# Four-block sequence model on one core: where the attention loop issues its strip matmuls, its maxima's transposes and its variances, and where the first expert tile's tokens lie

## The chip, the core and the metric

The kernel runs on one core of a Trainium2 chip. TensorE multiplies (PE, with PEld for its weight loads), VectorE (DVE) and ScalarE (ACT) do elementwise work and read PSUM, GpSimd (POOL) does elementwise work on SBUF and starts indirect DMAs, SyncE (SP) starts the other DMAs. Each engine takes its instructions in order; semaphores tie the engines to each other. The metric is the device time of one execution in microseconds, the median of three runs. All numbers are float32, so each matmul is recorded as two passes of TensorE (a transpose as one).

## What is computed

The input is `x` with 4 sequences of 512 tokens and 288 features, and one condition vector per sequence. Four blocks follow each other:

```python
x = x + ((z @ expm(A(cond))) - z) @ U.T           # z = x @ U, U from the QR of P
for block in (L1, L2, L3):                         # 16 heads of 18 features
    h = layernorm(x) * (1 + scale) + shift
    q, k, v = split(h @ Wqkv + bqkv)               # L2 also normalises each head of q and k
    x = x + gate * (softmax(q @ k.T * 18**-0.5) @ v @ Wproj + bproj)
    h = layernorm(x) * (1 + scale2) + shift2
    x = x + gate2 * mlp(h)                         # L3: the best 2 of 4 experts, weighted
```

The heads of L2 are normalised over their 18 features, so its q and k need a variance per head. L3's experts work on 19 tiles of 256 tokens, collected by routing.

## The kernel before

**Batches and steps.** The three attention blocks times four sequences make 12 batches, numbered n = 0 to 11 (n = 4 to 7 are L2, n = 8 to 11 L3). `attend(n, ...)` (L1207) runs 32 steps for a batch: 4 groups G of 4 heads, 8 steps s each. A step issues, in this order:

1. `maxima(ahead, mstep)` (L1119): four score matmuls (two heads, two passes each) into `p_s`, and on DVE a `tensor_reduce` to the row maxima `M`. It runs `LOOK = 10` steps ahead of the rest, so in step 22 of a batch it begins on the next batch's Q and K; in step 5 of a group it does the last piece (mstep 7) of the next group.
2. `weigh(G, s)` (L1139): the transposed scores of the present group into `p_st`, and the exponential on ACT. `p_s` and `p_st` share a PSUM tag of two buffers, so the next `p_s` can start once the last reduce is done.
3. in even steps `give_values()` (L1237): `p_av`, exponentials times values.
4. filling work: `left` grows by `total / 32`, plus 0.5 in odd steps and minus 0.5 in even ones; while it is positive, the next piece of the generator `fill` is issued and its cost is taken off.

Scores and the strip matmuls use 32 of the array's rows, so matmuls on different strips run side by side; `p_av` uses 128 rows and 32 columns, the rest all 128 rows.

`take_maxima(G + 1)` (L1130) transposes `M` on PE (four transposes into `p_m`; the last needs the reduces of msteps 6 and 7) and subtracts the result on DVE from Q (in the extra row that each head's Q has behind its 18 features). It is issued in step 6 of a group, between `weigh` and `give_values`.

**The filling work of batch n** is, in order: `project(n + 1)` (L1044) up to the point where it yields `None`; `finish(n - 1)` (L1180), the four output projections `p_o` with their gated additions; the rest of `project(n + 1)`; the transposes `p_t` for the MLP of batch n - 1; in batches 10 and 11 routing pieces. What is left in `fill` at the end of the 32 steps is issued there. After the steps, `mlp(n - 1)` runs.

`project` has nine jobs, five for q and k (`p_qk`, m = 0 to 4) and four for v (`p_v`), taken in pairs. A pair issues its dense matmuls (two blocks of 128 features), then the pending evictions of the pair before (`later`), then its two strip matmuls (the last 32 features, called tails here), then its first evictions. For L2 an eviction has three parts: square (ACT) and bias (DVE); `p_var` with logarithm and exponential (ACT); the scaling on DVE (`stage<-stage,qn_g,tmp`), the shift on POOL and the DMA to DRAM (`qd`). After the tails of qk 4 and v 0 come twelve DMAs: `qd` is read back into the padded Q and K of batch n + 1 (eight), and four zero rows. These DMAs are on SP's queue, in order with the transfers of attention's outputs (`o` to `od`), of the sums and of weights. Both q and k are read head by head with a stride of four, so each of K's four transfers contains rows of job m = 4; Q's four end with job m = 2.

PSUM tag `mm` has three buffers for `p_qk`, `p_v`, `p_var`, `p_m`, `p_o`, `p_t`. The SBUF tag `stage` has three buffers and `o`, attention's sums on their way to DRAM, three.

**After attention** two pools for the experts take the place of the pool `attn`. `tokens_T(0)` (L1427) transposes the first 256 tokens into `hTe`; `tile_pieces(t)` yields four times per tile, and at each yield `rest()` gets one slot: `slot(gen)` advances the routing of sequences 2 and 3 (`route`, L858) until a piece with a cost of 1.0 or more. All routing there is DVE chains with a few small matmuls (`p_r`, `p_logit`, `p_pos`, `p_T`).

Of the kernel before, what the change touches and what calls it, by code (L numbers as in the profile page):

```python
# [9 lines left out]
F32 = mybir.dt.float32  # L10
# [6 lines left out]
B, T, C = 4, 512, 288  # L17
NT = 4
KC, KP = 3, 96

KW, TAIL, STRIPS = 2, 32, 3
H, HD, HS = 16, 18, 32
VS = HD + 1
NG = 4
# [14 lines left out]
TS = 256  # L39
# [8 lines left out]
def cond_seq_kernel(ctx: ExitStack, tc: tile.TileContext, a: dict, out: bass.AP):  # L48
# [802 lines left out]
    def route(b):  # L851
# [23 lines left out]
        for j in range(NT):  # L875
            for k in range(KW + 1):
                r = slice(0, 128 if k < KW else TAIL)
                matmul(p[:, j * NE:(j + 1) * NE], h[r, k, j * 128:(j + 1) * 128], R["wg"][r, k, :],
                       start=(k == 0), stop=(k == KW))
            if j % 2:  # L880
                yield 1.6
        lg, rank, m, gt, ge, mx = (R[n] for n in ("lg", "rank", "m", "gt", "gte", "mx"))
        vector.tensor_copy(lg.rearrange("p j e -> p (j e)"), p[:, :n16])
        S4 = [128, NT, NE, NE]
# [33 lines left out]
        for j in range(NT):  # L918
            q = slice(j * NE, (j + 1) * NE)
            vector.tensor_tensor(low[:, q], wide(lo[:, q].rearrange("p (n o) -> p n o", o=1), [128, NE, 128]),  # L920
                                 wide(R["iota128"].rearrange("p (o k) -> p o k", o=1), [128, NE, 128]), ALU.is_equal)
            yield 0.6

        vector.tensor_mul(lg, lg, m)
        vector.tensor_reduce(mx, lg, AX.X, ALU.add)
# [102 lines left out]
    with tc.tile_pool(name="attn", bufs=2) as at:  # L1028
# [14 lines left out]

        def project(n, norm):  # L1044

            l, b = divmod(n, B)
            wqk, wv = WA[l][:2]
            h = hT[0]
            yield from layernorm(l, 0, b, h, norm)
            qd = scratch.tile([2 * H, HD, T], F32, tag="qd", name=f"qd{n}")  # L1050
            flat = qd.rearrange("h d t -> (h d) t")

            def qk_job(m):
                w = min(QP, QK - m * QP)
                cols = slice(m * QP, m * QP + w)
                p = pmm(f"p_qk{n}_{m}")

                def evict():
                    bias = QB[l][0:w, m:m + 1]
                    t = at.tile([QP, T], F32, tag="stage", name=f"stage{n}_{m}", bufs=3)[0:w]  # L1060
                    if l != 1:
                        scalar.activation(t, p[0:w], AF.Identity, bias=bias, scale=scol[0:w, m:m + 1])
                    else:
                        tmp = at.tile([128, 2, T], F32, tag="e", name=f"tmp{n}_{m}", bufs=6)
                        sq, rs = tmp[0:w, 0, :], tmp[0:w, 1, :]
                        scalar.activation(sq, p[0:w], AF.Square, bias=bias)
                        vector.tensor_scalar(t, p[0:w], bias, None, ALU.add)
                        yield 0.0
                        pv = pmm(f"p_var{n}_{m}")
                        matmul(pv[0:w], varsel.rearrange("p h d -> p (h d)")[0:w, 0:w], sq, start=True, stop=True)  # L1070
                        scalar.activation(rs, pv[0:w], AF.Ln, bias=eps5[0:w])
                        scalar.activation(rs, rs, AF.Exp, scale=-0.5)
                        yield 0.86
                        vector.scalar_tensor_tensor(t, t, gains[0][0:w, m:m + 1], rs, ALU.mult, ALU.mult)
                        nc.gpsimd.tensor_scalar(t, t, gains[1][0:w, m:m + 1], None, ALU.add)
                    dma(flat[cols], t)
                return p[0:w], 0.86, lambda k, r: (wqk[r, k, cols], h[r, k, :]), evict

            def v_job(j):
                p = pmm(f"p_v{n}_{j}")  # L1080

                def evict():
                    (scalar.copy if j % 2 else vector.tensor_copy)(
                        V[n % 2][:, j, :, 0:HD], p[:, :C].rearrange("p (h d) -> p h d", d=HD))
                    yield from ()
                return p[:, :C], 0.49, lambda k, r: (h[r, k, j * 128:(j + 1) * 128], wv[r, k, :]), evict

            jobs = [(qk_job, m) for m in range(NQ)] + [(v_job, j) for j in range(NT)]
            later = []
            for i in range(0, len(jobs), 2):  # L1090
                pair = []
                for job, arg in jobs[i:i + 2]:
                    p, cost, operands, evict = job(arg)
                    for k in range(KW):
                        matmul(p, *operands(k, slice(0, 128)), start=(k == 0), stop=False)
                        yield cost
                    pair.append((p, operands, evict))
                for e in later:
                    yield from e
                for q, (p, operands, evict) in enumerate(pair):  # L1100
                    matmul(p, *operands(KW, strip(q)), start=False, stop=True)

                later = [e for e in [evict() for p, operands, evict in pair] if next(e, None) is not None]
                yield 0.95
                if i <= NQ - 1 < i + 2:
                    for e in later:
                        yield from e
                    later = []

                    src = qd.rearrange("(s g i) d t -> s i d g t", s=2, i=4)  # L1110
                    for s, t in enumerate((Q[n % 2], K[n % 2])):
                        for q in range(4):
                            dma(t[q * HS:q * HS + HD], src[s, q])
                    for q in range(4):
                        dma(Q[n % 2][q * HS + HD:q * HS + VS], zero_row[q:q + 1].rearrange("a (g t) -> a g t", t=T))
                    there.add(n)
                    yield None

        def maxima(G, step):  # L1119
# [86 lines left out]

        def attend(n, fill, total, norms):  # L1207

            left = 0.0
            for step in range(8 * NG):  # L1210
                g, s = divmod(step, 8)
                G = NG * n + g
                ahead, mstep = divmod(8 * G + s + LOOK, 8)
                if ahead < NG * NB:
                    while ahead // NG not in there:
                        next(fill)
                    maxima(ahead, mstep)
                E.append(weigh(G, s))
                if s == 8 - 2 and G + 1 < NG * NB:
                    take_maxima(G + 1)  # L1220
                if s % 2 == 0:
                    give_values()
                left += total / (8 * NG) + (0.5 if s % 2 else -0.5)
                next(norms, None)
                while left > 0:
                    cost = next(fill, "end")
                    if cost == "end":
                        break
                    left -= cost or 0.0
                if s % 2:  # L1230
                    ready.append((G, s // 2))
            for _ in fill:
                pass
            for _ in norms:
                pass

        def give_values():  # L1237

            if not ready:
                return  # L1240
            G, c = ready.pop()
            if c == 0:
                PO[0] = pacc(f"p_av{G}")
            sum_values(G, PO[0], c, E[:2])
            del E[:2]
            if c == NT - 1:
                t = at.tile([128, T], F32, tag="o", name=f"o{G}", bufs=3)
                scalar.copy(t, PO[0])
                n, g = divmod(G, NG)
                if g == 0:  # L1250
                    S[n] = (scratch.tile([H, T], F32, tag="sd", name=f"sd{n}"),
                            scratch.tile([H, HD, T], F32, tag="od", name=f"od{n}"))
                dma(S[n][0][4 * g:4 * g + 4, :], t.rearrange("(h r) c -> h r c", r=HS)[:, HD])
                for h in range(4):
                    dma(S[n][1][4 * g + h], t[h * HS:h * HS + HD])
# [55 lines left out]
        for t in range(LOOK):  # L1311
            maxima(*divmod(t, 8))
            if t == 8:
                take_maxima(0)
            next(rest, None)
            next(new)
            if t == 5:
                projection_bias(0)
        for n in range(NB):
# [70 lines left out]
    with tc.tile_pool(name="moe", bufs=1) as pool, tc.tile_pool(name="moe2", bufs=2) as pool2:  # L1390
# [34 lines left out]
                gather(g, xtab if t >= EARLY else xtab[0:2 * T], idx[:, 2 * t + h:2 * t + h + 1])  # L1425

        def tokens_T(t):  # L1427
            h = HT[t] = pool2.tile([128, KW + 1, TS], F32, tag="hTe", name=f"hTe{t}")
            p, q = pmm(f"p_te{t}"), pmm(f"p_tf{t}")
            for i in range(2):  # L1430
                cols = slice(i * 128, (i + 1) * 128)
                for k in range(KW):
                    transpose(p[:, k * TS + i * 128:k * TS + (i + 1) * 128], XG[t, i][:, k * 128:(k + 1) * 128], ident)
                transpose(q[:XW - KW * 128, cols], XG[t, i][:, KW * 128:XW], ident)
            vector.tensor_copy(h[:, 0:KW].rearrange("p k n -> p (k n)"), p)
            scalar.copy(h[:XW - KW * 128, KW], q[:XW - KW * 128, :TS])

        def tile_pieces(t):
# [118 lines left out]
```

## Time and profile before

| | us |
|---|---|
| median of the three runs | 2061.03 (2056.3 to 2065.32) |
| the profiled execution | 2073.42 |
| its span on the core | 2071.7 |
| DVE busy, of it `TENSOR_REDUCE store<-p_s` x384 | 928.4, 470.3 |
| ACT busy, of it `ACTIVATE e<-p_st` x384 | 783.6, 392.7 |
| granted TensorE clock, mean | 0.954 |

The profiled execution is one run with the recorder on; views of its trace (timeline, waits, windows) count microseconds from its first instruction. PE's busy time is near the whole span in any case, since matmul records overlap; what a stage is bound by shows in the waits and the timeline. The first 213 us hold the rotation of block 0 and the first projections, the steps run from there to about 1655 us, the expert tiles from there to the end. The batches (first `p_st` to first `p_st` of the next) take between 86.9 us (n = 0, no MLP in it) and 143.2 us (n = 5).

### The profile page before, as it was taken

Reading aid. Unit: us, or ns where it says so; the run is one execution under the profiler, and the core shown is the slowest. Engines: PE = TensorE matmul, PEld = TensorE weight load, DVE = VectorE, ACT = ScalarE, POOL = GpSimd, SP = SyncE. Lnnn points to the kernel's source line nnn. Section 1 sums busy time; section 2 is a strip of 40 time slices with the busy share of each in tenths; the row PEclk is TensorE's granted clock in tenths of the full one; section 3 lists DMA queues with packets and bytes.
Section 4 is the critical chain, followed back from the end, with each engine's and each line's share of the span. In section 5 each row is a group of like instructions: output and inputs, shape, how many; then the busy total and the mean of one; then the engine's idle time right before and its main releaser. Section 6 shows DMA issues by size and latency. Waiting matters only on the chain. (4 is left out here: it accounts for less than half of the span.)

```text
span 2071.7 us, 26248 instructions
## 1 busy us (share of the span) xinstructions
PE 1887.7 (91%) x10269; PEld 935.6 (45%) x10269; DVE 928.4 (45%) x1953; ACT 783.6 (38%) x1169; POOL 251.9 (12%) x362
## 2 busy tenths in 40 slices
PE   6769879999999999899999999998987888999998
PEld 4544223343523434234234353333332266788886
DVE  6764646346164362552644626345576234211111
ACT  5122454444254343453544434434444222221221
POOL 1000010001010020010100000000000122233232
PEclk9578999999999999999999999999999689999999
DMA  3212152031131221511213112161212265576673
GB/s 97 71 40 62 36 147 84 22 89 36 25 85 30 70 62 42 136 42 54 72 26 77 42 54 81 21 134 35 83 46 66 86 222 167 182 242 200 211 241 97
DMA packets 89419, 187.23 MB, mean 90 GB/s; under 512 B 25453, under 2 KB 50456, under 8 KB 86802
## 3 DMA queue, kind: packets, MB, share of 16 engines
q1 hardware_dynamic: 77462, 103.39, 19.1%
q0 software_dynamic: 11248, 79.79, 11.9%
q10 hardware_dynamic: 584, 2.36, 0.3%
q8 instruction: 81, 1.33, 0.3%
q14 instruction: 44, 0.36, 0.1%
HBM read 152.49 MB, written 55.45 MB: 100 GB/s over the span
## 5 line engine op out<-in xcount | busy, mean ns | idle before, releaser
L60 ACT ACTIVATE e<-p_st 128x1024 f32<-128x1024 f32 x384 | 392.7, 1023 | 650.7 <-PE p_st L60 646.3
L60 DVE TENSOR_REDUCE store<-p_s 128x2 f32<-128x1024 f32 x384 | 470.3, 1225 | 364.5 <-PE p_st L60 320.7
L60 PE MATMUL p_s<-store 32*128 32x512 f32 x1536 | 442.2, 648 | 82.5 <-DVE store L60 81.3
L60 PE MATMUL p_st<-store 32*128 32x512 f32 x1536 | 445.7, 659 | 0.9 <-DVE store L60 0.9
L60 PEld LDWEIGHTS p_s<-store 32*128 32x128 f32 x1536 | 120.0, 185 | 315.3 <-DVE store L60 228.2
L60 PE MATMUL p_av<-e,store 128*32 128x512 f32 x1536 | 212.8, 627 | 2.2 <-ACT e L60 2.2
L60 PE MATMUL p_he<-hTe,store 128*128 128x256 f32 (+1 forms) x1026 | 188.4, 390 | 4.2 <-DVE hTe L60 4.2
L60 PE MATMUL p_ye<-store,hide 128*128 128x288 f32 x684 | 171.4, 409 | 0.0
L60 PEld LDWEIGHTS p_he<-hTe,store 128*128 128x128 f32 (+1 forms) x1026 | 151.4, 191 | 37.7 <-issue 13.6
L695 POOL TENSOR_TENSOR x<-x,gated 128x288 f32<-128x288 f32 x80 | 63.9, 799 | 841.6 <-DVE gated L60 841.6
L60 PE MATMUL p_qk<-hT,wqk 128*126 128x512 f32 (+1 forms) x360 | 163.1, 622 | 0.3 <-DVE store L60 0.3
L60 ACT ACTIVATE hide<-p_he,store 128x256 f32<-128x256 f32 x171 | 68.5, 478 | 245.1 <-PE p_he L60 244.3
L60 PE MATMUL p_h<-hT,w 128*128 128x512 f32 (+1 forms) x432 | 153.5, 610 | 5.2 <-DVE store L60 5.2
L60 PEld LDWEIGHTS p_ye<-store,hide 128*128 128x128 f32 x684 | 128.2, 190 | 36.7 <-ACT hide L60 2.3
L60 PE MATMUL p_y<-w,hid 128*128 128x288 f32 x576 | 141.8, 407 | 0.0
L60 DVE TENSOR_TENSOR gated<-p_y,gate 128x288 f32<-128x288 f32 x32 | 14.6, 457 | 283.0 <-PE p_y L60 283.0
L60 PEld LDWEIGHTS p_y<-w,hid 128*128 128x128 f32 x576 | 108.8, 190 | 35.5 <-issue 6.1
L60 PEld LDWEIGHTS p_st<-store 32*128 32x128 f32 x1536 | 118.2, 187 | 12.1 <-issue 9.1
L60 PEld LDWEIGHTS p_h<-hT,w 128*128 128x128 f32 (+1 forms) x432 | 62.1, 189 | 95.1 <-issue 84.9
L60 PE MATMUL p_o<-wp,oc 126*128 126x288 f32 (+1 forms) x288 | 99.4, 468 | 1.3 <-DVE oc L60 1.3
L60 PEld LDWEIGHTS p_qk<-hT,wqk 128*126 128x126 f32 (+1 forms) x360 | 47.1, 178 | 95.9 <-issue 94.3
L60 DVE COPY hTe<-p_te 128x512 f32<-128x512 f32 x19 | 13.1, 690 | 169.2 <-PE p_tf L60 117.8
(248 smaller groups left out, 1728.8 us busy)
## 6 DMA issues: line engine op xcount, KB each, us to landing
store<-qd SPq DMA_DIRECT2D x96, 144.0 KB
qd<-stage SPq DMA_DIRECT2D x48, 252.0 KB
od<-o SPq DMA_DIRECT2D x192, 36.0 KB
rd<-rd SPq DMA_DIRECT2D x12, 576.0 KB
oc<-od SPq DMA_DIRECT2D x24, 252.0 KB
rb<-rd SPq DMA_DIRECT2D x24, 252.0 KB
etab<-in_L_cond_w_dram SPq DMA_DIRECT2D x4, 1296.0 KB
etab<-in_L_cond_w_dram SPq DMA_DIRECT2D x8, 576.0 KB
```

The lines of the kernel that those rows point to most:

```text
L60: ins = f(*args, **kw)
L695: nc.gpsimd.tensor_add(x[b][:, j, :], x[b][:, j, :], t)
```

## The change

- `project` yields the word "strips" ahead of its tails. `attend` stops filling there, and issues the tails in the next step, right behind `weigh` and ahead of `give_values`.
- `take_maxima(G + 1)` moves from step 6 (behind `weigh`) to step 5, behind its filling work; `left` is reduced by 0.6 in such a step.
- For L2 (`l == 1`) the pending evictions of qk 4 are no longer drained at once behind its tails: the drain and the twelve DMAs (`send`) come one pair later, behind the dense matmuls of v 1 and v 2.
- `stage` has four buffers, `o` two.
- `hTe0` lies in a buffer of `wqk` in place of the experts' pool.
- In `route`, for sequences 2 and 3, the first half of the logits costs 0.8 and the last piece of `low` 1.0.

```diff
@@ route
             if j % 2:
-                yield 1.6
+                yield 0.8 if b >= 2 and j < NT - 1 else 1.6
@@
-            yield 0.6
+            yield 1.0 if b >= 2 and j == NT - 1 else 0.6
@@ project
-                    t = at.tile([QP, T], F32, tag="stage", name=f"stage{n}_{m}", bufs=3)[0:w]
+                    t = at.tile([QP, T], F32, tag="stage", name=f"stage{n}_{m}", bufs=4)[0:w]
@@
+            def send():
+
+                src = qd.rearrange("(s g i) d t -> s i d g t", s=2, i=4)
+                for s, t in enumerate((Q[n % 2], K[n % 2])):
+                    for q in range(4):
+                        dma(t[q * HS:q * HS + HD], src[s, q])
+                for q in range(4):
+                    dma(Q[n % 2][q * HS + HD:q * HS + VS], zero_row[q:q + 1].rearrange("a (g t) -> a g t", t=T))
+                there.add(n)
@@
                 for e in later:
                     yield from e
+                if l == 1 and i <= NQ + 1 < i + 2:
+                    send()
+                    yield None
+                yield "strips"
                 for q, (p, operands, evict) in enumerate(pair):
                     matmul(p, *operands(KW, strip(q)), start=False, stop=True)
 
                 later = [e for e in [evict() for p, operands, evict in pair] if next(e, None) is not None]
                 yield 0.95
-                if i <= NQ - 1 < i + 2:
-                    for e in later:
-                        yield from e
-                    later = []
...
+                if l != 1 and i <= NQ - 1 < i + 2:
+                    send()
                     yield None
@@ attend
-            left = 0.0
+            left, strips = 0.0, False
@@
                 E.append(weigh(G, s))
-                if s == 8 - 2 and G + 1 < NG * NB:
-                    take_maxima(G + 1)
+                if strips:
+                    left -= next(fill)
+                    strips = False
                 if s % 2 == 0:
                     give_values()
-                left += total / (8 * NG) + (0.5 if s % 2 else -0.5)
+                take = s == 7 + 8 - LOOK and G + 1 < NG * NB
+                left += total / (8 * NG) + (0.5 if s % 2 else -0.5) - (0.6 if take else 0.0)
                 next(norms, None)
                 while left > 0:
                     cost = next(fill, "end")
-                    if cost == "end":
+                    strips = cost == "strips"
+                    if cost == "end" or strips:
                         break
                     left -= cost or 0.0
+                if take:
+                    take_maxima(G + 1)
                 if s % 2:
                     ready.append((G, s // 2))
@@ give_values
-                t = at.tile([128, T], F32, tag="o", name=f"o{G}", bufs=3)
+                t = at.tile([128, T], F32, tag="o", name=f"o{G}", bufs=2)
@@ tokens_T
-            h = HT[t] = pool2.tile([128, KW + 1, TS], F32, tag="hTe", name=f"hTe{t}")
+            if t:
+                h = pool2.tile([128, KW + 1, TS], F32, tag="hTe", name=f"hTe{t}")
+            else:
+                h = wattn.tile([128, KW + 1, QK], F32, tag="wqk", name="hTe0")[:, :, 0:TS]
+            HT[t] = h
@@
-            vector.tensor_copy(h[:, 0:KW].rearrange("p k n -> p (k n)"), p)
+            vector.tensor_copy(h[:, 0:KW], p.rearrange("p (k n) -> p k n", k=KW))
```

More of the change, by code (lines that the diff above doesn't have):

```diff
@@ L1104, in project @@
                 yield 0.95
-                if i <= NQ - 1 < i + 2:
-                    for e in later:
-                        yield from e
-                    later = []
[L1110 to L1116, printed above, removed]
+                if l != 1 and i <= NQ - 1 < i + 2:
+                    send()
                     yield None
@@ L1315, in cond_seq_kernel @@
             next(rest, None)
-            next(new)
+            if next(new) == "strips":
+                next(new)
             if t == 5:
```

## The prediction

> **What bounds the kernel now.** I read the page's busy shares and slices first, then the waits of PE, then the timeline of single steps.
>
> ```profile
> PE 1887.7 (91%) x10269; PEld 935.6 (45%) x10269; DVE 928.4 (45%) x1953; ACT 783.6 (38%) x1169; POOL 251.9 (12%) x362
> PE   6769879999999999899999999998987888999998
> PEclk9578999999999999999999999999999689999999
> ```
>
> PE is nearly full from slice 6 to the end, and its clock sags around slices 32 and 33 (1605 to 1710 us). So any stall of PE goes straight to the end. The waits of PE from 480 to 1640 us (total, times, longest):
>
> ```profile
> PE p_s L60 <- DVE store L60: 62.2, 90, 3.8
> PE p_t L60 <- DVE xn L60: 6.5, 7, 1.1
> ```
>
> The score matmuls wait for the reduce of the step before. The timeline of PE in batch 7 gives the rhythm (start, busy, engine):
>
> ```profile
> 1111.72 0.70 PE L60 MATMUL p_s<-store 32*128 32x512 f32 x2
> ...
> 1114.18 0.70 PE L60 MATMUL p_s<-store 32*128 32x512 f32 x2 [0.32 <-DVE store L60]
> ...
> 1115.34 1.98 PE L60 MATMUL p_qk<-hT,wqk 128*126 128x512 f32 x4
> 1117.26 0.70 PE L60 MATMUL p_s<-store 32*128 32x512 f32 x2
> ```
>
> From 1111.72 to 1114.18 is 2.46 us: scores 1.07 us, reduce 1.23, hand-overs. That is the floor of a step. The next step has two dense `p_qk` and takes 3.08: PE bound. **A step takes the larger of 2.46 us and the sum of its PE rows.** From starts in the timeline: scores 1.07, a dense 512-column matmul 0.86 (two passes of 0.429), `p_av` 1.06, `p_o` 1.84, a pair of tails behind scores 0.86, behind dense work 1.05, and a change of array shape about 0.2 (the next pass starts 0.522 after the last in place of 0.429, and the second pass 0.53 after the first). Walking all 32 steps of batch 4 so gives 127.6 us against 132.8 in the trace; the rest are waits that stand in the timeline one by one (variances, `xn`, the gap ahead of the MLP).
>
> **Steps.** I put the program order of both kernels through that rule. The change spreads unevenly: when "strips" ends an odd step's filling, that step is left at the floor with about 1.4 us of PE unused, and the next, even step carries tails, `p_av` and dense work. Batch 7 by the rule: steps 11 to 15 were 2.9 + 2.5 + 2.6 + 3.4 + 3.8 and become 2.5 + 3.9 + 2.7 + 2.5 + 2.5, which gains 1.1; but steps 20 to 27, 4.0 + 2.5 + 3.3 + 2.7 + 2.7 + 2.2 + 2.7 + 2.2, become 4.0 + 2.7 + 4.0 + 2.5 + 2.7 + 2.7 + 2.5 + 2.6, which loses 1.4, and the other steps lose 1.5 (0.3 in 0 to 10, 0.5 in 16 to 19, 0.7 after the last score step). The transposes cost 0.2 above the floor in both places: in step 6 as 1.07 + 0.6 + 1.0, in step 5 because the last of the four waits for that step's own reduce. The 0.6 taken off in four steps per batch leaves a piece (`p_t`) for the end. Differences of the sums: batch 0 +0.5; 1, 2 +1.9 each; 3 to 6 +3.5 each; 7, 8 +1.7 each (rounded rows above: 1.8); 9 +0.4; 10 +0.7; 11 +2.0. **Sum +24.8.** Taken back: the last `p_t` now fill the gap in which the MLP's first matmul waited 0.9 for a reduce, 8 x 0.9 = -7.2; waits for `xn` shrink 4 x 0.4 = -1.6.
>
> Here a rule can be set against the rows. The Trainium skill, "TensorEngine Tiling (Array Packing)", Tiling Modes, says that a change of tiling mode drains TensorE. The row agrees (0.2 us). In the program order there are 1147 such changes before and 1125 after. By the rule alone 22 x 0.2 = -4.4 us; by the steps, +24.8, since most removed changes lie in steps that wait for DVE anyway. I take the steps.
>
> **Variances (batches 3 to 6).** In step 9 both `p_var` stood together, the second 1.05 us behind its PSUM buffer; steps 14 to 16 lost about 1.45 more, with DVE behind two scalings and two evictions. Both pairs are now steps apart: 4 x -2.5 = -10. Against it, `p_v` 1 and 2 hold two of the three `mm` buffers during `p_o`, so the second `p_o` of step 23 waits for a 0.45 us eviction: 4 x 0.75 = +3. In batch 5 the DVE queue stood at `oc<-oc,rb`, then at a full `stage`, PE idled 3.75 us and the clock fell: 143.2 against 132.8 us. With `var` 1 a step earlier and four `stage` buffers I leave 1.5 of these 10.7: -9.2. Two `o` buffers cost nothing: the DMAs of one leave within 3 us of its copy, and a group lasts about 22; without that cover ACT's copy, with all exponentials behind it, would wait.
>
> **The late Q and K.** This decides. The timeline of batch 4, whose filling is batch 5's projection:
>
> ```profile
> 748.99 1.08 PE L60 MATMUL p_var<-tmp,varsel 72*72 72x512 f32 x2
> ...
> 751.49 0.75 DVE L60 SCALAR_TENSOR_TENSOR stage<-stage,qn_g,tmp 72x512 f32<-72x512 f32 x1 [1.16 <-ACT tmp L60]
> ...
> 752.39 1.56 POOL L1075 TENSOR_SCALAR stage<-stage,qn_b 72x512 f32<-72x512 f32 x1 [4.81 <-issue]
> ...
> 753.98 0.29 SPq L1076 DMA_DIRECT2D qd<-stage  x1
> ...
> 756.40 1.39 SPq L1113 DMA_DIRECT2D store<-qd  x4
> ...
> 763.86 0.70 PE L60 MATMUL p_s<-store 32*128 32x512 f32 x2
> ```
>
> After the last `p_var` (step 17) the scaling starts at 751.49; shift, write and four K reads follow. The trace's landing events put the first two K reads at 759.71 and 760.71, **9.2 us after the scaling starts**. The scores of step 22, which read them, come at 763.86: 3.1 us to spare. After the change this `p_var` stands in step 19, behind two `p_v`. The scaling is issued in step 21, on DVE behind that step's reduce, so 2.4 us into it; step 22 would begin 3.5 us into step 21, but K lands at 2.4 + 9.2 = 11.6. PE's next instruction is the score matmul waiting for K, and behind it in order stand `p_st`, `p_av` and all else; ACT and DVE run dry with it. **11.6 - 3.5 = 8.1 us in each of batches 3 to 6: +32.4.** Bounds: 6.5 if DMAs or SP are freer than in the row, 10 if SP has output transfers ahead.
>
> A stall also cools the clock (us, PE busy and so on, then granted clock):
>
> ```profile
> 866.50:869.95 3.45, 0.60 (x2) 0.00 (x0) 2.28 (x4) 0.00 (x0) 1.56 (x1) 1.00 0.34 108
> 869.95:876.77 6.82, 5.92 (x20) 2.21 (x20) 3.26 (x4) 1.02 (x1) 0.00 (x0) 0.50 0.25 67
> ```
>
> PE was busy 0.60 of 3.45 us, and half clock followed for 6.8 us. The Trainium skill, "TensorE: Matmul & The Clock Gate", Part 1, speaks against this change: an idle window of about 3.4 us halves the clock, a busy one restores it. By the rule 3.4 us at half clock follow each stall, 1.7 lost, 4 x 1.7 = 7; the rows show 6.8 us here and 10.2 after another wait in that batch, about 3 lost: 4 x 3 = **+12**. I take the rows; ends 0 and 24.
>
> **Experts.** `hTe` had to wait for `o` to reach DRAM, since the pools share memory (timeline of PE):
>
> ```profile
> 1659.09 3.78 PE L60 MATMUL p_he<-hTe,store 128*128 128x256 f32 x8 [4.24 <-DVE hTe L60]
> 1663.52 0.48 PE L60 MATMUL p_r<-ident,xn 128*128 128x128 f32 x1 [0.65 <-POOL xn L859]
> ...
> 1695.97 1.94 PE L60 MATMUL p_T<-low,arena 128*32 128x128 f32 x32 [5.11 <-DVE arena L60]
> ```
>
> With its own buffer `p_he` starts near 1655.8. That alone would be lost at `p_r`, but the program order also puts POOL's four additions (0.65 each) ahead of its gathers, which still wait for `o`; `p_r` ends near 1660.2 in place of 1667.4, so -7. `p_logit` in one slot brings `p_pos` ahead of a `p_ye` of 4.5 us, and `low` (2.5 us of DVE) runs beneath the second: the two waits of `p_T` (5.1 and 3.4) shrink to about 1.5 and 1, -6. One of the 13 I leave to later waits: **-12** (ends -3 and -16). The weights of tile 1 land near 1675, ahead of need.
>
> **Batch 11's end** ran at half clock from 1614 to 1648 us (2.08 us for a pair of `p_st` that takes 1.07 elsewhere), because steps 19 to 22 do little. They do little after too; the likeliest is the same, -1; without it -14.
>
> **Sum:** 24.8 - 7.2 - 1.6 - 10 + 3 - 9.2 + 32.4 + 12 - 12 - 1 = +31.2 us on the profiled 2073.4. That execution lies 12.4 above the median; the difference carries over: 2061 + 31 = **2092 us**, 1.5% slower.
>
> **Rivals.** (1) K is in time. Place: step 22 of batches 3 to 6; if the stall and its clock cost less than 13.2 / 4 = 3.3 us per batch, the rest wins; at none, 2061 - 13 = 2048. For it: 3.1 us to spare today. Against: the wait stands in the new program order, and scaling, shift, write and reads are in series. 8%. (2) The clock, once low, stays low, as in batch 11, because `p_o` at half rate does not wake it: 6 more per stall, 2116. For it: 34 us at 1614. Against: `p_s` is issued beside it here. 14%. (3) Batch 11 escapes its half clock, 2078. 15%. (4) The stalls come out at their low end and the experts at their high end, 2065, not told from no change (within 0.5%, 10 us, is what a measurement can't tell). 8%. The forecast itself: 55%.
>
> **Range** 2067 to 2114: bounds of stall, clock and experts, with rival 3 inside and 2 at its edge. Faster 0.08 (rival 1), same 0.08 (rival 4), slower 0.84 (the rest).
>
> **What will show it.** `p_s` waiting for DMA `store<-qd` four times by about 7 us, near step 22 of batches 3 to 6, each followed by half clock; no 1.05 us wait at `p_var`; batch 5 no longer 10 us longer than batch 4; `p_he` first near 4 us earlier against the end of `p_av`; waits of `p_T` under 2 us. Four waits under 3 us, or K landing less than 6 us after the scaling, would make the prediction wrong.

## The result, and the profile after

The changed kernel takes 2126.68 us, median of four runs (2118.35 to 2132.40), against 2063.18 us (2056.30 to 2075.61) for the kernel before: ratio 1.0283, 95% interval 1.0242 to 1.0325. The direction was forecast, the size was not: +31 was forecast, some +60 came. The profiled execution of the changed kernel took 2129.09 us (span 2127.4, mean clock 0.940), 55.7 more than the profiled one of before.

The page of the changed kernel, busy line and slices:

```profile
PE 1915.4 (90%) x10269; PEld 945.2 (44%) x10269; DVE 931.5 (44%) x1953; ACT 783.4 (37%) x1169; POOL 254.5 (12%) x362
PE   6779888999998989979989999999987989999998
PEclk9569999999999999999999999999988779999999
```

The instruction counts are the same, so the change added no work. PE's busy time is 27.7 us longer, at a lower mean clock (0.940 against 0.954). The clock now sags over four late slices, where it was two before. The waits of PE in the stretch of the steps, 480 to 1700 us (total, times, longest):

```profile
PE p_s L60 <- DVE store L60: 65.2, 106, 1.9
PE p_s L60 <- DMA store<-qd: 23.9, 4, 6.1
PE p_m L60 <- DVE store L60: 14.6, 19, 1.3
```

The second line was not there before: four waits of the scores for K, one in each of batches 3 to 6. The timeline of batch 4, at the same place as in the prediction:

```profile
775.48 1.02 PE L60 MATMUL p_var<-tmp,varsel 72*72 72x512 f32 x2
...
781.21 0.74 DVE L60 SCALAR_TENSOR_TENSOR stage<-stage,qn_g,tmp 72x512 f32<-72x512 f32 x1
...
783.69 0.29 SPq L1077 DMA_DIRECT2D qd<-stage  x1
...
785.73 1.39 SPq L1094 DMA_DIRECT2D store<-qd  x4
...
788.99 2.04 PE L60 MATMUL p_s<-store 32*128 32x512 f32 x2 [5.91 <-DMA store<-qd]
```

Step 21 began at 778.9, so the scaling is 2.3 us into it, as forecast. The score matmul starts 7.8 us after the scaling, when the first K read lands (788.86 by the trace's landing events). PE had stood for 5.9 us. What that does to the clock (us, length, then busy time and instructions of PE, PEld, DVE, ACT, POOL, then granted clock, DMA share, GB/s):

```profile
781.78:785.20 3.42, 0.75 (x5) 0.42 (x4) 1.28 (x3) 0.00 (x0) 2.32 (x2) 1.00 0.15 41
785.20:788.61 3.41, 0.00 (x0) 0.00 (x0) 0.00 (x0) 0.00 (x0) 0.00 (x0) 0.50 0.35 82
788.61:792.02 3.41, 3.03 (x8) 1.03 (x8) 0.00 (x0) 0.00 (x0) 0.00 (x0) 0.50 0.45 93
792.02:795.40 3.38, 3.38 (x19) 0.72 (x16) 1.77 (x3) 1.02 (x1) 0.00 (x0) 0.50 0.00 0
```

Of 10.2 us at half clock some 3.4 fall into the stall and cost nothing; some 6.8 fall on work, which takes nearly twice its time there (a `p_av` 1.94 us, 1.06 before the stall), and cost 3.4.

By batch (first `p_st` of one to first `p_st` of the next; the last column is the sum of the prediction's own terms for it):

| batch | before | changed | difference | forecast |
|---|---|---|---|---|
| start to first `p_st` | 213.5 | 214.7 | +1.2 | 0 |
| 0 | 86.9 | 86.4 | -0.5 | +0.5 |
| 1 | 130.7 | 138.2 | **+7.5** | +1.0 |
| 2 | 132.5 | 135.3 | +2.8 | +1.0 |
| 3 to 6 together | 542.8 | 578.0 | +35.2 | +37 |
| 7, 8 | 126.7, 126.7 | 127.5, 127.5 | +0.8 each | +0.8 each |
| 9, 10 | 89.8, 100.2 | 93.3, 104.5 | **+7.8** | +1.1 |
| 11 to its last `p_st` | 101.0 | 99.4 | -1.6 | +1.0 |
| from there to the last matmul | 410.3 | 411.9 | **+1.6** | -12 |

So the four batches that were expected to decide came out as forecast in their sum. In part that is luck: the waits were smaller than forecast, and less was gained elsewhere in these batches. What failed stands in the three bold rows: batch 1, batches 9 and 10, the experts. Together they are 26.8 us over their forecast. The other rows nearly cancel.

Batch 1, timeline of the changed kernel (`md` is the last modulation, a shift and a scale; `mrow` gets its rows):

```profile
299.19 0.33 PE L60 MATMUL p_modT<-ident,md 128*128 128x128 f32 x1 [2.01 <-ACT md L60]
299.87 0.29 SPq L324 DMA_DIRECT2D mrow<-md  x1
...
323.17 0.35 SPq L1166 DMA_DIRECT2D sums<-sd  x1
...
324.77 0.55 DVE L60 RECIPROCAL sums<-sums 128x64 f32<-128x64 f32 x1 [5.11 <-DMA sums<-sd]
325.24 0.63 DVE L60 TENSOR_TENSOR store<-store,p_m 128x512 f32<-128x512 f32 x1
...
327.05 1.37 PE L60 MATMUL p_st<-store 32*128 32x512 f32 x4 [3.58 <-DVE store L60]
```

It is read from the bottom: PE waits 3.6 us for DVE's subtraction in Q, DVE stood 5.1 us at the reciprocal, the reciprocal waited for its sums, and these came late because SP had sent the modulation rows (`mrow`), and behind them all weights of the next layer, only from 299.87 on. The same transfers and the same reciprocal in the kernel before:

```profile
286.87 0.24 SPq L324 DMA_DIRECT2D mrow<-md  x1
...
310.33 0.34 SPq L1161 DMA_DIRECT2D sums<-sd  x1
...
320.10 0.54 DVE L60 RECIPROCAL sums<-sums 128x64 f32<-128x64 f32 x1
```

### The profile page after: what moved, and what is told of

The parts are those of the page before. It is cut to its first block, busy times and chain, and to the rows that moved or that the text cites. A ratio compares the mean times of both kernels' runs of the same rounds, so it can differ in the third digit from the quotient of the medians.

```text
span 2127.4 us, 26237 instructions
## 1 busy us (share of the span) xinstructions
PE 1915.4 (90%) x10269; PEld 945.2 (44%) x10269; DVE 931.5 (44%) x1953; ACT 783.4 (37%) x1169; POOL 254.5 (12%) x362
## 5 line engine op out<-in xcount | busy, mean ns | idle before, releaser
L60 PE MATMUL p_s<-store 32*128 32x512 f32 x1536 | 454.6, 661 | 107.2 <-DVE store L60 81.8
L60 PE MATMUL p_st<-store 32*128 32x512 f32 x1536 | 456.2, 671 | 3.6 <-DVE store L60 3.6
L60 PE MATMUL p_qk<-hT,wqk 128*126 128x512 f32 (+1 forms) x360 | 168.1, 632 | 0.3 <-DVE store L60 0.3
L695 POOL TENSOR_TENSOR x<-x,gated 128x288 f32<-128x288 f32 x80 | 63.5, 794 | 870.4 <-DVE gated L60 870.4
L60 PEld LDWEIGHTS p_st<-store 32*128 32x128 f32 x1536 | 120.0, 190 | 12.9 <-issue 8.3
L60 PEld LDWEIGHTS p_av<-e,store 128*32 128x32 f32 x1536 | 31.0, 111 | 154.9 <-issue 152.2
```

Source lines behind the costliest of these rows:

```text
L60: ins = f(*args, **kw)
L695: nc.gpsimd.tensor_add(x[b][:, j, :], x[b][:, j, :], t)
```

## The experiments

All ratios are to the kernel before on the same chip. Each kernel was also profiled once; batch lengths are from that profile.

**1. The early drain and send put back in the changed kernel.**

```diff
-                if l == 1 and i <= NQ + 1 < i + 2:
-                    send()
-                    yield None
                 yield "strips"
...
-                if l != 1 and i <= NQ - 1 < i + 2:
+                if i <= NQ - 1 < i + 2:
+                    for e in later:
+                        yield from e
+                    later = []
                     send()
                     yield None
```

> The change with one part undone: for L2 the evictions of qk 4 are again drained right behind their strip matmuls and the twelve DMAs follow at once; all else as changed. Theory 'late K': of the loss, about 24 us are four waits for K and about 20 us the half clock behind them, so this kernel comes to 2080 to 2096 us, ratio to before 1.008 to 1.016; no score matmul waits more than 2 us for K, and batches 3 to 6 take 131 to 137 us each. Theory 'spread': the new spread of the filling work costs the time by itself, and this kernel stays above 1.02 of before.

Measured: 2098.13 us, ratio 1.0134 (1.0097 to 1.0172). Of the waits for K three are left, of 0.2 to 0.8 us; batches 3 to 6 take 135.2, 133.5, 139.9 and 135.8 us, 33.6 less together than in the changed kernel. The theory "late K" holds, with the median 2 us and batch 5 3 us over its bounds, and "spread" falls. About half of the loss goes with the late send; batch 1 stays at 139.3.

**2. The late send alone in the kernel before** (the reverse of the edit above).

> The kernel before with one part added: for L2 the drain and the twelve DMAs come one pair later, behind the dense matmuls of v 1 and v 2. Here the write of job 4 is issued in step 20 (step 21 in the changed kernel), so theory 'late K' expects four waits of the score matmuls for K of 3 to 5 us, each followed by 3 to 10 us of half clock: +25 to +40 us, ratio 1.012 to 1.020. Theory 'spread': less than +12 us, ratio under 1.006.

Measured: 2096.40 us, ratio 1.0143 (1.0113 to 1.0173): the size as expected, the way only in part. Waits of PE, 480 to 1700 us:

```profile
PE p_s L60 <- DMA store<-qd: 4.7, 5, 1.3
```

K is one step less late here than in the changed kernel, and the wait is 1.1 to 1.3 us a batch, not 3 to 5. The rest of the 5.5 to 7.3 us that batches 3, 4 and 6 lose stands in fuller steps 19 to 22 (`p_v` and `p_o` come together; step 22 takes 6.1 us, at half clock, against 2.7); it was not taken apart further.

**3. The strip matmuls alone** in the kernel before (the "strips" lines of the diff).

> The kernel before with only the strip matmuls moved behind the next step's transposed scores (and filling stopped ahead of them). Step sums by the rule of the prediction: +27.6 us, 2.5 in each batch 1, 2, 7 and 8 and 3.5 in 3 to 6. With the gaps ahead of the MLP that the later pieces fill, about -7: +15 to +28 us, ratio 1.007 to 1.014. Theory 'clock': thin steps also cool the clock, and it comes to more than +30 us. A rival that the moves cost nothing: within 0.5%.

Measured: 2086.09 us, ratio 1.0079 (1.0050 to 1.0109), inside what the step sums gave. But in its profile batches 1 and 7 lost 5.4 and 5.7 us, not 2.5, and batch 5 was 8.7 shorter than before (134.5), which no sum had: that the median fits is in part chance. Windows of batch 7 around step 12 (columns as above):

```profile
1142.80:1146.20 3.40, 1.76 (x20) 0.46 (x16) 2.51 (x4) 1.62 (x2) 0.00 (x0) 1.00 0.43 119
1146.20:1149.60 3.40, 3.40 (x12) 0.96 (x12) 1.92 (x3) 1.02 (x1) 0.00 (x0) 0.50 0.00 1
1149.60:1153.00 3.40, 3.40 (x12) 0.52 (x10) 0.30 (x1) 1.45 (x2) 0.00 (x0) 0.50 0.39 126
```

In the first window PE never waits longer than 1.3 us; two floor steps leave it busy for 1.76 of 3.40 us. 6.8 us at half clock follow, and they fall on step 12, which carries `p_av`, strips and dense work. It need not come so. Steps 10 and 11 stand at the floor in all of batches 1 to 8 here, but step 12 takes 7.21 us in batches 1 and 7 alone, 3.92 in 2 and 8, 4.78 in 3 to 6. Batch 3, at the same steps, keeps full clock behind a window as thin:

```profile
606.89:610.30 3.41, 1.78 (x20) 0.69 (x18) 2.52 (x5) 1.29 (x2) 0.00 (x0) 1.00 0.25 80
610.30:613.71 3.41, 3.41 (x23) 0.96 (x16) 2.94 (x4) 2.18 (x3) 1.56 (x1) 1.00 0.08 26
```

**4. More work in these thin steps.** As 3, and where filling stops ahead of the strips with time left, four matmuls that nobody reads:

```diff
+                    if strips and left > 0.4:
+                        keep_busy(f"busy{G}_{s}")
...
+        def keep_busy(name):
+            p = pmm(name)
+            for j in range(4):
+                matmul(p[:, j * 128:(j + 1) * 128], ident, ident, start=True, stop=True)
```

> As before_strips, with four matmuls of 128 columns more (ident times ident, read by nobody) wherever the filling stops ahead of the strip matmuls with more than 0.4 of a step's work left, 33 times; the step sums rise by 5.1 us. In before_strips two floor steps in a row, 10 and 11 of batches 1 and 7, were followed by 6.8 us at half clock (step 12 at 7.21 us, step 16 at 4.75). Theory 'thin steps cool the clock': step 12 of batches 1 and 7 comes to 3.5 to 4.0 us, these batches to 129 to 131.5 and the kernel to -4 to +4 us of before_strips although it does more. Rival: the half clock there is chance; step 12 stays at 7.2 in one of the two, and the kernel is 3 to 6 us slower than before_strips.

Measured: 2080.70 us, ratio 1.0056 (1.0032 to 1.0079). Step 12 takes 3.92 us in both batches (7.21 in each without), and the windows there read

```profile
1144.14:1147.56 3.42, 3.19 (x26) 1.66 (x20) 1.94 (x3) 1.02 (x1) 0.00 (x0) 1.00 0.27 72
1147.56:1150.97 3.41, 3.41 (x22) 0.68 (x18) 1.71 (x2) 2.36 (x3) 0.00 (x0) 1.00 0.23 73
```

So a thin step can cost twice: its idle time, and half clock for the full step behind it. Batch 1 came to 133.3, over the 131.5 that was expected; batch 7 came to 130.7, and lost 1.6 us again in step 22, at half clock. The median is 5 us below 3, though the intervals overlap. Since six of eight batches escaped in 3 too, these two alone do not exclude chance; the count of windows in the last section says more.

**5. The maxima's transposes alone** in the kernel before (`take`, with its 0.6).

> The kernel before with only the transposes of the maxima in step 5 (and 0.6 less filling there). Step sums +5.1 us, less about 7 for the gaps ahead of the MLP and with the two variances of jobs 0 and 1 two steps apart (step 9 and 11), about 1 us in each of four batches: ratio 0.995 to 1.002. Theory that waiting for the own step's reduce is what makes the changed kernel slow (its four transposes wait 18 us in 25 places): ratio above 1.006.

Measured: 2102.11 us, ratio 1.0136 (1.0078 to 1.0195): +35 us by the medians, +28 by the ratio, where -10 to +4 was expected. The transposes are not what is slow. Timeline of batch 4, step 12 (7.87 us, 3.23 before):

```profile
744.41 1.85 SPq L1076 DMA_DIRECT2D qd<-stage  x2
746.98 0.75 DVE L60 TENSOR_SCALAR stage<-p_qk,qkb 126x512 f32<-126x512 f32 x1 [3.35 <-DMA qd<-stage]
...
748.91 1.09 PE L60 MATMUL p_s<-store 32*128 32x512 f32 x2 [4.21 <-DVE store L60]
```

The moved fillings bring the biases of jobs 2 and 3 before the writes of jobs 0 and 1 have left `stage`; with three buffers DVE waits, and the reduce behind it, and PE.

**6. The same with four `stage` and two `o` buffers.**

> The kernel before with the transposes of the maxima in step 5 and with the buffer counts of the change (stage four, o two). Alone, the move cost 35 us, of which step 12 of batches 3, 4 and 6 took 4.6 us each with DVE waiting for a write of stage. Theory 'stage': that wait goes, step 12 is back under 4 us, batch 5 comes to 133 to 137 us, and the kernel to +8 to +20 us, ratio 1.004 to 1.010. Rival 'own reduce': the last transpose's wait for its own step's reduce carries the loss, and it stays above 1.012.

Measured: 2067.72 us, ratio 1.0011 (0.9983 to 1.0039); batches 3 to 6 at 135.8, 134.0, 137.4 and 135.3. The theory "stage" holds and was too cautious: the buffers take back all that can be told. In the change these two belong together: without the buffers the move costs as much as the late send. Which of the two buffer counts it needs was not tried apart; the wait above is for `stage`.

**7. The buffer counts alone.**

> The kernel before with only the buffer counts: stage four, o two. The prediction's step gave -9.2 us in batch 5 with nothing elsewhere: ratio 0.993 to 0.9975, batch 5 at 133 to 136 us (143.2 before). Rival 'o': with two buffers ACT's copy of o waits for the transfers of the one before, the exponentials behind it, and the kernel is not faster.

Measured: 2064.88 us, ratio 0.9986 (0.9951 to 1.0021); batch 5 takes 142.9 us as before. The step of the prediction that put batch 5's loss on a full `stage` is wrong. DVE in step 12 of batch 5, in the kernel before and then with the buffers:

```profile
865.73 0.69 DVE L60 TENSOR_TENSOR oc<-oc,rb 126x512 f32<-126x512 f32 x1 [2.31 <-DMA rb<-rd]
...
868.91 0.75 DVE L60 TENSOR_SCALAR stage<-p_qk,qkb 126x512 f32<-126x512 f32 x1 [1.17 <-POOL stage L1075]
```

```profile
868.87 0.69 DVE L60 TENSOR_TENSOR oc<-oc,rb 126x512 f32<-126x512 f32 x1 [3.51 <-DMA rb<-rd]
869.47 0.75 DVE L60 SCALAR_TENSOR_TENSOR stage<-stage,qn_g,tmp 126x512 f32<-126x512 f32 x1
870.14 1.41 DVE L60 TENSOR_SCALAR stage<-p_qk,qkb 126x512 f32<-126x512 f32 x2
```

The 1.17 us that DVE waited for `stage` is gone, but the wait for `rb`, the factors of batch 4, is 3.51 where it was 2.31, and step 12 takes 6.8 us as before (6.9). The rival "o" has nothing for it either: no copy of `o` waits longer.

**8. The zero rows held back.** As 1, with the four transfers of zero rows pinned in the program's order, since in the changed kernel three of them stood on SP ahead of `mrow` and waited 7.4 us for batch 0's last scores:

```diff
-                    dma(Q[n % 2][q * HS + HD:q * HS + VS], zero_row[q:q + 1].rearrange("a (g t) -> a g t", t=T))
+                    tc.keep_in_program_order(dma(Q[n % 2][q * HS + HD:q * HS + VS], zero_row[q:q + 1].rearrange("a (g t) -> a g t", t=T)))
```

> The changed kernel with the early drain and send (as in after_early_send), and the four transfers of zero rows held in program order with the weight loads, so that none of them can stand on SP's queue ahead of batch 1's modulation rows and weights. Theory 'queue': in batch 1 the reciprocal no longer waits for its sums on DVE, and batch 1 falls from 139.3 us to 130.5 to 133.5; in all 6 to 9 us less than after_early_send, ratio to before 1.009 to 1.011. Theory 'spread': batch 1 is slow by its thin steps and their clock, and stays above 137 us.

Measured: 2103.12 us, ratio 1.0202 (1.0134 to 1.0270). A miss: batch 1 takes 137.5, and SP now waits 9.4 us for the modulation (`md`) itself. The zero rows had only waited beside it. In batches 3 to 6 the pinned rows come late in turn (four waits of `p_s`, 15.9 us).

**9. The rows in time.** As 1, with the 0.6 only from batch 1 on, so that batch 0 ends its last modulation in step 27, as before, and not in 31:

```diff
-                left += total / (8 * NG) + (0.5 if s % 2 else -0.5) - (0.6 if take else 0.0)
+                left += total / (8 * NG) + (0.5 if s % 2 else -0.5) - (0.6 if take and n else 0.0)
```

> The changed kernel with the early drain and send (as in after_early_send), and with the 0.6 taken off the filling only from batch 1 on. Then batch 0 ends its last modulation in step 27 as before the change, and not in step 31. Theory 'late rows': SP stood for these rows with the weights, the sums and the reciprocal behind it; here batch 1's reciprocal waits for nothing, step 6 of batch 1 takes under 3.6 us (7.1 in the changed kernel), and batch 1 comes to 130.5 to 133.5 us in place of 139.3: ratio to before 1.008 to 1.012. Theory 'thin steps': batch 1 is slow by its floor steps and their clock and stays above 136 us.

Measured: 2072.75 us, ratio 1.0037 (0.9997 to 1.0077). Its timeline, the lines of batch 1 again:

```profile
287.88 0.24 SPq L324 DMA_DIRECT2D mrow<-md  x1
...
310.31 0.34 SPq L1166 DMA_DIRECT2D sums<-sd  x1
...
318.77 0.54 DVE L60 RECIPROCAL sums<-sums 128x64 f32<-128x64 f32 x1
```

The reciprocal waits for nothing, batch 1 takes 130.8 us (139.3 in 1). The median falls by more than this one batch, 25 us: batch 11 of the profile is 8 shorter as well (see below), and what the rest is was not taken apart.

**10. The rows in time, the late send kept.**

> The changed kernel with the 0.6 taken off the filling only from batch 1 on, and nothing else: the late send stays. Theory 'late K': its cost, 1.47% by after_early_send against the changed kernel, stands apart from batch 1 and comes on top of early_send_credit (1.0037): ratio 1.015 to 1.021; batch 1 at 130 to 133 us, four waits of score matmuls for K of 5 to 6.5 us, batches 3 to 6 at 141 to 147 us. Rival: the two losses fed each other (a cooled clock, a late queue), and the late K costs under 1% here, ratio under 1.013.

Measured: 2105.84 us, ratio 1.0219 (1.0143 to 1.0295), four waits for K of 23.2 us together, batches 3 to 6 at 142.6, 143.0, 146.7 and 145.5, batch 1 at 131.2. The ratio is just over the 1.021 of the theory and its interval leaves the rival's 1.013 out: the late K costs here about what it cost in the changed kernel. By the medians of 9 and 10 it is 33 us (38 by the ratios), by 1 and the changed kernel 29 (31).

**11 and 12. The experts' part alone** in the kernel before (`hTe0` and the two routing costs), and the same with batch 11's reciprocal issued first:

```diff
-            for c in "BBIBBBIBBB":
+            for c in "IBBBBBIBBB":
```

> The kernel before with only the experts' part: tokens of tile 0 in a buffer of wqk, and the two routing costs. The prediction gave this part -12 us (-3 to -16), ratio 0.994. Theory 'queue': freed early, the eight writes of routed tokens now stand on SP ahead of the write of the reciprocals, which then shares the DMA engines with the gathers; the output factors come late, DVE waits for them ahead of the routing chain, and the two waits of p_T stay at 5 and 3.4 us: -5 to +3 us, ratio 0.9975 to 1.0015.

> As before_experts, with batch 11's reciprocal and its two transfers issued ahead of routing's first piece, so that they stand ahead of the eight writes on SP. Theory 'queue': the factors land 8 us or more earlier, the first wait of p_T falls from 5 to under 2.5 us, and the kernel is 3 to 9 us faster than before_experts: ratio to before 0.993 to 0.998. Rival: the routing chain on DVE is as long in any order, and both come out within 2 us of each other.

Measured: 2072.85 us, ratio 1.0027 (1.0000 to 1.0053), and 2065.06 us, 0.9986 (0.9953 to 1.0018), 7.8 us apart. Timeline of the first:

```profile
1668.65 0.45 SPq L1168 DMA_DIRECT2D rd<-sums  x1
...
1681.52 0.59 SPq L1170 DMA_DIRECT2D rd<-rd  x1
...
1688.54 0.69 DVE L60 TENSOR_TENSOR oc<-oc,rb 126x512 f32<-126x512 f32 x1 [4.95 <-DMA rb<-rd]
...
1695.94 1.30 PE L60 MATMUL p_T<-low,arena 128*32 128x128 f32 x20 [7.31 <-DVE arena L60]
```

and of the second:

```profile
1657.15 0.32 SPq L1168 DMA_DIRECT2D rd<-sums  x1
...
1661.04 0.59 SPq L1170 DMA_DIRECT2D rd<-rd  x1
...
1693.15 1.08 PE L60 MATMUL p_T<-low,arena 128*32 128x128 f32 x32 [2.27 <-DVE arena L60]
```

With `hTe0` free early, eight writes of routed tokens come ahead of `rd<-sums` on SP, and the gathers start meanwhile. The next transfer, which needs that write, goes 12.9 us after it, against 3.9. `rb` lands late, DVE waits with `oc<-oc,rb` ahead of the routing chain, and `p_T` waits 7.3 us. With the reciprocal first that wait is 2.3, but DVE now stands 5.2 us at the reciprocal and `p_r` waits 6.2 for POOL's additions. From batch 11's last `p_st` to the end both take as long as before (410.3): 410.6 and 412.7 us. Each wait that goes is followed by others of about its size. The 7.8 us between the medians therefore do not lie in this stretch, as far as the profiles show: there batch 11 took 100.5 us in the first and 90.5 in the second, with 37.5 and 20.5 at half clock, which the last section takes up. So the median does not confirm the theory; the trace confirms its queue.

**13 and 14. PE kept busy at the end of batch 11**, with four `stage` and two `o` buffers, and without:

```diff
+                if n == NB - 1 and 19 <= step <= 24:
+                    keep_busy(f"busy{G}_{s}")
```

> As before_stage4, with the same four matmuls added to steps 19 to 24 of batch 11 (step sums +4.3 us). Theory 'thin steps': the 34 us at half clock behind step 22 do not come; from batch 11's first transposed scores to its last 88 to 95 us (101.0 in the profile of before), and the kernel is within 2 us of before_stage4 or up to 10 us faster. Rival: the stretch behind step 22 is thin by the exponentials and falls to half clock in any case; 4 us slower than before_stage4.

> The kernel before with only the four matmuls more in steps 19 to 24 of batch 11, buffers as before. before_stage4 came to 0.9986 (not told from 1) and before_stage4_busy to 0.9954. Theory 'busy': the added matmuls carry the gain, 0.994 to 0.998, batch 11 at 85 to 90 us. Rival 'buffers': without them the ratio is 0.999 or above.

Measured: 2060.11 us, ratio **0.9954 (0.9933 to 0.9976)**, and 2066.42 us, 0.9982 (0.9947 to 1.0016). The first beats both kernels: 7.8 us under before, 67 under the changed one. Which of its parts carries it stays open: neither alone can be told from no change, and its profile was also the one in which batch 5 took 135.4 us in place of 143.

**15. The same in 9.**

> As early_send_credit, with four matmuls of 128 columns more in steps 19 to 24 of batch 11. Theory 'thin steps': batch 11 takes 84 to 92 us in place of 91.6 to 99.5, runs lie closer together, ratio 0.997 to 1.002, so that nothing is left of the loss of the changed kernel but the late K and the late rows. Rival: the loss left is in the experts and in batches 2 to 6, and the ratio stays above 1.003.

Measured: 2078.26 us, ratio 1.0057 (1.0026 to 1.0088). Batch 11 takes 86.9 us, but the kernel is no faster than 9: the rival is right, a loss of about 9 us is left in batches 2 to 6 (135.3, 135.0, 133.5, 139.1, 136.3), in 9 and 10 (93.3, 104.6) and in the experts.

## Why the prediction was wrong

The forecast was 32 us short. The three rows make 26.8 of it and the step from the profile to the median 8. Three terms of the sum failed, each by what it left out: batch 1 (+1.0, what stands behind a late piece on SP), batches 9 and 10 (+1.1, the clock), the experts (-12, SP's order). One by one:

- **The late Q and K: right, and a little too large.** Place, chain and number of waits are as forecast. 8.1 us a wait was 5.9, since the first score matmul needs only the first K read (7.8 us after the scaling, where 9.2 to the second was charged) and PE has work until 4.2 us into the step, not 3.5: +32.4 came to 23.9. The half clock behind was +12 and is 4 x 3.4 = 13.6. Experiments 1, 9 and 10 put both together at 29 to 38 us.
- **The step sums: right where nothing else happens.** +1.7 less 0.9 for the MLP's gap was forecast for batches 7 and 8; +0.8 came in both. The strips alone gave +19 us of median by experiment 3, within the range of its sum, though with more lost in batches 1 and 7 and less in batch 5.
- **"The 0.6 taken off leaves a piece (`p_t`) for the end": the failing step of batch 1.** In batch 0 what is left over is a modulation. Its rows gate SP, SP gates the weights and the sums, and DVE waits for these: +7.5 where +1.0 was forecast. Experiment 9 shows it, 8 clears the zero rows of it. The profile before shows the queue: SP already waited 5.1 us for `md` there, with weights and sums behind it.
- **The steps of batches 9 and 10 were costed by idle time alone, without their clock.** They lose 7.8 us where 1.1 was forecast. Four stretches at half clock of 3.4 to 6.8 us stand between 1430 and 1608 us, where there were two of 3.4 before. Experiments 3 and 4 show that thin steps can cool the clock. In batch 9 (+3.5) the trace has that: 6.8 us at half clock behind a floor step. It was not tried, and it is not certain to come: experiment 9 took 90.0 us for this batch, and 15, the same program up to batch 11, 93.3. Batch 10 (+4.3) is another case. Its first stretch at half clock, of 6.8 us, follows a window that PE fills:

```profile
1574.41 3.76 PE L60 MATMUL p_logit<-arena,hT 128*128 128x4 f32 x23
```

```profile
1573.70:1577.10 3.40, 3.40 (x28) 2.59 (x20) 1.56 (x2) 1.34 (x2) 0.00 (x0) 1.00 0.00 0
1577.10:1580.50 3.40, 3.40 (x18) 1.80 (x22) 0.15 (x1) 0.09 (x1) 0.00 (x0) 0.50 0.00 0
```

With one more behind them these are the 24 routing matmuls of four columns (the views as above: timeline, then windows). Before, they stood in two groups, six us apart from start to start, and no half clock followed either. All eight profiles with the maxima moved (among them 5, which moves nothing else) have them together and half clock right behind. So the moved fillings, not a floor step, bring this stretch. The strips alone give batch 10 as much (104.9 us in 3), and the added matmuls of 4 hardly shorten it (104.5), so the parts of its loss were not taken apart.

- **The experts, -12: the waits of `p_T` did not shrink.** The first half of the step came: PE's wait ahead of `p_he` fell from 4.2 to 0.6 us. But in the changed kernel the first `p_T` waits 5.5 us, because DVE stands 3.1 us at `oc<-oc,rb`, the second 3.4 as before, and nothing of the gain is left at the last matmul (+1.6). The prediction followed PE, DVE and POOL and left SP's order out; experiments 11 and 12 show the queue and the trade of one wait for the next.
- **Batch 5, -9.2: wrong cause.** The full `stage` was the smaller wait (experiment 7); in experiment 3, with three buffers, DVE waits 0.6 us for `rb`, and the batch takes 134.5 us. Most of the loss is the clock behind the stall, and that is chance in part: the programs of 7 and 13 are the same up to batch 11, `rb` is late in both (3.5 and 2.9 us), and batch 5 took 142.9 us with 17.1 us at half clock in one, 135.4 with none in the other. In the changed kernel `rb` is late by 2.7 us, and no half clock follows there either. The waits at `p_var` are gone, as forecast. Variances, batch 5 and `p_o`'s buffer together were put at -16.2; what is left of batches 3 to 6 without K, clock, steps and the small gaps is 35.2 - 23.9 - 13.6 - 14 + 3.6 + 1.6 = -11.1.
- **"The difference carries over" to the median: 8 us off.** The profiles differ by 55.7 us, the medians by 63.5. One likely reason, not shown: the execution profiled before held 34 us at half clock in batch 11, which other executions of the same kernel need not have.
- The Trainium skill, "TensorE: Matmul & The Clock Gate", Part 1, was read for idle gaps of about 3.4 us. The traces show that less can suffice: in experiment 3 one window with PE busy for 52% of it was followed by half clock, one with the same share was not. The rule's concern spoke against the change in more places than the prediction used it.

## What to carry to other kernels

When filling work is spread anew, follow the last pieces of each stretch to whoever takes their result: a queue that is served in order turns a piece that is four steps late into late weights and late sums. Where PE has just enough to do, count what a thin step can do to the clock of the step behind it as well as its own idle time, and leave a floor step some dense work. A buffer count that gains nothing by itself can save some 30 us once a move has been made: try the two as a pair before dropping either.

## What the runs showed of the hardware that was not expected

- How thin a window must be. The granted clock changes in steps of 3.41 us, so the traces can be counted in such windows. In the 17 profiles, between the first and the last `p_st`, windows at full clock were followed by half clock as follows, by PE's busy share: under 45%, 67 of 67; 45 to 60%, 67 of 123; 60 to 82%, 41 of 1071; 82 to 98%, none of 1880.
- A window that PE fills can lose the clock too. Of 3713 windows with more than 98%, 32 were followed by half clock, and all 32 held matmuls of one or four columns: seventeen the biases and gains in batch 2 (1x1 in the rows), fifteen `p_logit` in batches 10 and 11.
- Half clock comes in pieces of 3.4 us, and in batch 11 it can hold on although PE is busy throughout: 34 us in the profile before, 44 in the changed one. Of 14 profiles of kernels without the added matmuls in batch 11, seven took 99 us or more for it and seven 92 or less, without regard to the edit; the three with them took 85.7, 86.9 and 90.7. Three profiles are few, so that the added work prevents it is likely, not shown.
- The same 128 x 64 write of reciprocals was followed by its reader after 3.3 to 5.0 us in nine of the ten profiles in which two gathers stood ahead of it (7.8 in the tenth), and after 11.7 to 13.8 us in all seven in which three to five gathers and the eight writes did. The load of the DMA engines meanwhile does not tell them apart: their share was 1.05 over the 3.9 us of experiment 12 and 0.87 over the 12.9 us of 11. What counts is what was queued ahead, as far as these runs show.
